# A two-layer decoder in one kernel: a shorter block table, ranks taken from logits, and the blocks' normalisation worked out in pairs

## The chip, the cores and the metric

One Trainium2 chip, one core. The metric is the device time of one execution in microseconds, the median of three executions: 1794.66 (1793.82 to 1794.86) for the kernel before. The profile that is quoted below comes from another execution of the same kernel, with a time of its own.

## The reference, cut to what matters

Thirty-two batches of 100 tokens with 256 features pass six stages. Every stage adds its input and ends in a layer norm without gain:

```python
x = _layernorm(x + _L0_attn_ref(x, ...), axis=-1)
x = _layernorm(x + _L0_xattn_ref(x, ctx_1024, ctx_1024, fside_BxSxS2_0, ...), axis=-1)
x = _layernorm(x + _L0_ffn_ref(x, ...), axis=-1)
x = _layernorm(x + _L1_attn_ref(x, ...), axis=-1)
x = _layernorm(x + _L1_xattn_ref(x, ctx_1024, ctx_1024, ...), axis=-1)
x = _layernorm(x + _L1_ffn_ref(x, ...), axis=-1)
```

The change is in the last stage, a mixture of eight experts of which each token takes one:

```python
logits = x_flat @ Wg + bg
probs = jax.nn.softmax(logits, axis=-1)
assignments = jnp.argmax(probs, axis=-1)
h = jnp.einsum('nd,edh->neh', x_flat, W1) + b1[None]
h = jax.nn.gelu(h, approximate=False)
eo = jnp.einsum('neh,ehd->ned', h, W2) + b2[None]
selected = jnp.take_along_axis(eo, assignments[:, None, None], axis=1)[:, 0, :]
w = jnp.take_along_axis(probs, assignments[:, None], axis=1)
out = (w * selected).reshape(N, T, d)
```

## The kernel before

**Two layers of attention, in slots.** Nearly all of the time goes into self-attention and cross-attention of 32 batches in two layers. Their work is written out by hand: `at(slot, place, do)` puts a step at one of four places of a slot, and `run_slots` (L677) issues slot after slot. The order of each engine's instructions is the order of these calls; no scheduler moves them.

**Routing, beside the last attention slots.** When a batch has left the second layer's cross-attention, `router` (L518) makes its logits. Batches are routed in groups of four; the last groups are 28 to 30, and 31 alone (`group_of`, L582). For each group `centred_logits` (L592) subtracts the largest logit, `exponentials` (L598) takes exp on ScalarE, and `one_hot` (L601) forms the shares and marks the expert with the largest one, by a product with `rank` so that one alone is marked. `ahead_of` (L615) adds the marks into `sofar`; `counted` (L622) counts on TensorE how many tokens of the same expert come before a token; `rows_of` (L627) makes a row number of that; `send` (L641) scatters the batch's rows with an indirect DMA from GpSimd into `regions` in DRAM, in which each expert has an area of its own. A row has 258 numbers: 256 features, the share, and the token's number.

**The block table.** `block_table` (L652) cuts the regions into 32 blocks of 128 rows. From the counts of the eight experts it works out, on all 128 partitions and for all 32 blocks along the free axis (128 x 256 elements), at which row each block begins and which expert it belongs to. The result is `table`, whose first partition is read into registers by SyncE, TensorE and VectorE.

**The blocks.** After the slots come the 32 blocks (L828). For block i, `load_block` (L778) reads two registers and loads the rows `xb` and the expert's first weights `wb`, ten blocks ahead; `turn_block` (L790) transposes on TensorE and copies on ScalarE (`bxT`), two ahead; `first_layer` (L798) makes four products and two Gelu activations (`bhT`), one ahead; `second_layer` (L809) makes the second product (`bo`) and then on VectorE adds the bias `b2` (L817), multiplies by the share and adds the residual (L818), and takes mean and variance (L77, L79); GpSimd works out the scale as (variance + margin) to the power -0.5 (L81, L82). `store_block` (L821) follows one block later: VectorE centres and scales (L86), and GpSimd scatters 128 rows into the output (L637). `b2`, 1 MB with its copies for all partitions, is loaded by SyncE ahead of the first block (L773). Each of the PSUM tiles of the blocks has two buffers; `xb` and `wb` have twelve.

The order on GpSimd is thus margin, power, scatter of the block before, margin, power, scatter, and so on. An engine runs its instructions in order: one that waits holds up all behind it.

Of the kernel before, what the change touches and what calls it, by code (L numbers as in the profile page):

```python
# [10 lines left out]
F32 = mybir.dt.float32  # L11
# [7 lines left out]
E = 8  # L19
# [5 lines left out]
GROUP = 4  # L25
ROW = D + 2
# [5 lines left out]
NO_TOKEN = 1.0e6  # L32
LAYER = (0, SLOTS * B + 23)
COLUMNS = ("parity", "l0s_bq", "l0s_bk", "l0s_bv", "l0x_bq", "l0x_bk", "l0x_bv", "l1x_bq", "l1x_bk", "l1x_bv")
ROWS = ((("l0s_bo", D), ("l0x_bo", D), ("dscale", 1), ("ffn_g", D), ("ffn_b", D)),
        (("l1s_bo", D), ("l1x_bo", D), ("bg", E), ("rank", E), ("base", E), ("order", BLOCKS)))
# [20 lines left out]
def decoder_kernel(ctx: ExitStack, tc: tile.TileContext, a: dict, out: bass.AP):  # L57
# [10 lines left out]
    table = state.tile([P, 2, BLOCKS], I32, name="table")  # L68
# [19 lines left out]
    with ExitStack() as att:  # L88
# [21 lines left out]
        nc.vector.tensor_copy(x_all[:, :, D + 1], ids)  # L110
        no_token = const.tile([P, ROW], F32, name="no_token")
        nc.gpsimd.memset(no_token, 0.0)
        nc.gpsimd.memset(no_token[:, D + 1:], NO_TOKEN)
# [341 lines left out]
        def plan_batch(l, b):  # L455
# [103 lines left out]
            if l == 0:  # L559
                at(start + 8, 2, keep("ln_n", lambda: layer_norm_scale(sm, xs[b], 0.001, "n", f"n_{b}")))  # L560
                at(start + 9, 3, feed_forward_input)
                at(start + 11, 3, lambda: transpose_rows(t["xn"], "n", tag, dst=xnT[:, :, b, :]))
            else:
                at(start + 9, 0, keep("x3T", lambda: transpose_rows(xs[b], "m", tag)))
                at(start + 11, 1, router)
                first, n = group_of(b)
                if b == first + n - 1:
                    for do, s, place in ((centred_logits, 11, 3), (exponentials, 12, 1), (one_hot, 12, 3),
                                         (ahead_of, 13, 3), (counted, 15, 0), (rows_of, 15, 3)):
                        at(start + s, place, lambda do=do: do(first, n))  # L570
                    for i in range(n):
                        at(start + 16 + i, 1, lambda i=i: send(first + i))
# [9 lines left out]
        def group_of(b):  # L582

            if b == B - 1:
                return b, 1
            first = b // GROUP * GROUP
            return first, min(GROUP, B - 1 - first)

# [3 lines left out]
        def centred_logits(first, n):  # L592
            routed["col"] = sm.tile([S, GROUP], F32, tag="col", name=f"col_{first}")[:, :n]
            lg = routed["lg"] = routed["logits"][:, :n, :]
            nc.vector.tensor_reduce(routed["col"], lg, AX.X, ALU.max)
            nc.vector.tensor_tensor(lg, lg, over_experts(routed["col"]), ALU.subtract)
# [4 lines left out]
        def one_hot(first, n):  # L601

            lg, col = routed["lg"], routed["col"]
            nc.vector.tensor_reduce(col, lg, AX.X, ALU.add)
            nc.vector.reciprocal(col, col)
            nc.vector.tensor_tensor(lg, lg, over_experts(col), ALU.mult)
            top = x_all[:, first:first + n, D]
            nc.vector.tensor_reduce(top, lg, AX.X, ALU.max)
            hot = routed["hot"] = w2.tile([S, GROUP, E], F32, tag="hot", name=f"hot_{first}")[:, :n, :]
            nc.vector.tensor_tensor(hot, lg, over_experts(top), ALU.is_equal)  # L610
            nc.vector.tensor_tensor(hot, hot, c["rank"][:S].unsqueeze(1).to_broadcast([S, n, E]), ALU.mult)
            nc.vector.tensor_reduce(col, hot, AX.X, ALU.max)
            nc.vector.tensor_tensor(hot, hot, over_experts(col), ALU.is_equal)
# [38 lines left out]
        def block_table():  # L652

            ps = bank("counts")[:, :E]
            nc.tensor.matmul(ps, lhsT=ones[:S, :], rhs=sofar, start=True, stop=True)
            full = w1.tile([P, E, B], F32, tag="full", name="full")
            nc.vector.tensor_tensor(full[:, :, :PER_EXPERT], ps.unsqueeze(2).to_broadcast([P, E, PER_EXPERT]),
                                    c["order"][:, :PER_EXPERT].unsqueeze(1).to_broadcast([P, E, PER_EXPERT]), ALU.is_gt)
            n = sm.tile([P, E], F32, tag="tb_n", name="tb_n")
            nc.vector.tensor_reduce(n, full[:, :, :PER_EXPERT], AX.X, ALU.add)  # L660
            upto = sm.tile([P, E], F32, tag="tb_upto", name="tb_upto")
            nc.vector.tensor_copy(upto[:, 0:1], n[:, 0:1])
            for e in range(1, E):
                nc.vector.tensor_tensor(upto[:, e:e + 1], upto[:, e - 1:e], n[:, e:e + 1], ALU.add)
            nc.vector.tensor_scalar(upto, upto, float(P), None, ALU.mult)
            nc.vector.tensor_scalar(n, n, -float(P), float(B * S), ALU.mult, ALU.add)
            past = w1.tile([P, BLOCKS, E], F32, tag="past", name="past")
            nc.vector.tensor_tensor(past, c["order"].unsqueeze(2).to_broadcast([P, BLOCKS, E]),
                                    upto.unsqueeze(1).to_broadcast([P, BLOCKS, E]), ALU.is_ge)
            col = sm.tile([P, BLOCKS], F32, tag="tb_col", name="tb_col")  # L670
            nc.vector.tensor_reduce(col, past, AX.X, ALU.add)
            nc.vector.tensor_scalar(table[:, 1, :], col, float(E - 1), None, ALU.min)
            nc.vector.tensor_tensor(past, past, n.unsqueeze(1).to_broadcast([P, BLOCKS, E]), ALU.mult)
            nc.vector.tensor_reduce(col, past, AX.X, ALU.add)
            nc.vector.tensor_tensor(table[:, 0, :], col, c["order"], ALU.add)
# [77 lines left out]
        at(LAYER[1] + 2, 3, load_second_weights)  # L753
        for i in range(FILLS):
# [6 lines left out]
        run_slots()  # L761
        block_table()

    with ExitStack() as moe:
        mw = moe.enter_context(tc.tile_pool(name="mw", bufs=1))
        m2 = moe.enter_context(tc.tile_pool(name="m2", bufs=2))
        m4 = moe.enter_context(tc.tile_pool(name="m4", bufs=4))
        m12 = moe.enter_context(tc.tile_pool(name="m12", bufs=12))
# [3 lines left out]
        b2 = mw.tile([P, E, D], F32, name="b2")  # L772
        nc.sync.dma_start(b2, a["b2"].to_broadcast([P, E * D]).rearrange("p (e d) -> p e d", e=E))  # L773
        y_all = mw.tile([P, BLOCKS, D], F32, name="y_all")
        to_all = mw.tile([P, BLOCKS], I32, name="to_all")
        blocks = [{} for _ in range(BLOCKS)]

        def load_block(i):  # L778
            t = blocks[i]
            why = "the table's rows and experts are within these bounds for any counts"  # L780
            first = nc.values_load(table[0:1, 0, i:i + 1], engines=(mybir.EngineType.SP,), min_val=0,
                                   max_val=(BLOCKS_AT_MOST - 1) * P, skip_runtime_bounds_check_because=why)
            t["e"] = nc.values_load(table[0:1, 1, i:i + 1], engines=(mybir.EngineType.SP, mybir.EngineType.PE, mybir.EngineType.DVE),
                                    min_val=0, max_val=E - 1, skip_runtime_bounds_check_because=why)
            t["x"] = m12.tile([P, ROW], F32, tag="xb", name=f"xb_{i}")
            nc.sync.dma_start(t["x"], regions[bass.ds(first, P), :])
# [22 lines left out]
        def second_layer(i):  # L809
# [5 lines left out]
            nc.vector.tensor_copy(to_all[:, i:i + 1], t["x"][:, D + 1:])  # L815
# [86 lines left out]
```

## Time and profile before

| what | us |
|---|---|
| median of three executions | 1794.66 |
| time of the profiled execution | 1794.34 |
| its span, first to last instruction | 1792.6 |
| last batch's logits on VectorE (L525) | 1688.11 |
| block table's first step on VectorE (L657) | 1691.93 |
| last output of `block_table` (L675) | 1696.58 to 1696.77 |
| first block's transposes on TensorE (L794) | 1702.02 |
| first block's bias on VectorE (L817) | 1708.51 |
| last scatter of rows into the output begins | 1785.46 |

Read it from the outside in. TensorE is busy for 96% of the span, with a granted clock of 0.98 on average, and 85% of the chain that ended last is TensorE's: that is the two layers of attention. The last hundred microseconds are another matter: there TensorE has idle stretches, and the order of GpSimd and VectorE sets the pace. A column "idle before" tells how long an engine had nothing to do before a group, and the arrow whom it waited for; a time on the GpSimd line is rougher than on the others.

### The profile page before, as it was taken

What the parts mean: (1) busy time and instruction counts of PE and PEld (TensorE: products, weight loads), DVE (VectorE), ACT (ScalarE), POOL (GpSimd) and SP (SyncE); (2) the same over time, 40 slices, a digit from 0 to 9 for tenths busy, and PEclk for the clock granted to TensorE, in tenths of its full rate; (3) what the DMA queues carried; (4) which work ended last, traced back from release to release, by engine and by line L of the source; (5) the groups of instructions that cost most, each with busy time, mean ns of one, the idle gap of its engine ahead of it and who ended that gap; (6) DMA issues with size and microseconds to landing.
All of it is one profiled execution on the core that took longest, in us unless ns stands there. A gap on an engine that the chain in (4) does not pass through costs nothing.

```text
span 1792.6 us, 52296 instructions
## 1 busy us (share of the span) xinstructions
PE 1712.5 (96%) x20797; PEld 1303.7 (73%) x20797; DVE 1294.8 (72%) x3846; ACT 914.7 (51%) x2285; POOL 1114.9 (62%) x1685
## 2 busy tenths in 40 slices
PE   8999999999999999998899999999999999999595
PEld 6777777777777777776667777777777777776384
DVE  5667776777777776786577777877777777866576
ACT  3555555555555555554345555555555555554242
POOL 1565666666666666664166666676766666665467
PEclk9999999999999999999899999999999999999898
DMA  4000232233313231210100000000000000000182
GB/s 156 13 30 21 79 83 69 57 82 79 81 49 83 79 82 54 68 33 10 64 2 18 19 15 23 18 28 18 20 18 28 18 15 23 19 28 12 54 253 92
DMA packets 60592, 89.38 MB, mean 50 GB/s; under 512 B 5723, under 2 KB 43101, under 8 KB 60222
## 3 DMA queue, kind: packets, MB, share of 16 engines
q1 hardware_dynamic: 56334, 78.91, 15.6%
q0 software_dynamic: 3584, 6.59, 1.2%
q8 instruction: 165, 2.70, 0.6%
q14 instruction: 77, 0.63, 0.1%
q10 hardware_dynamic: 432, 0.53, 0.1%
HBM read 52.09 MB, written 34.84 MB: 48 GB/s over the span
## 4 chain that ended last, share of the span: by engine, by line
PE 85%; POOL 5%; DVE 5%; issue 2%; ACT 1%; DMA 0%; SPq 0%; POOLq 0%; DVEq 0%; ACTq 0%
PE r_t_x L362 15%; PE sc_x L265 11%; PE r_v L507 9%; PE r_k L496 9%; PE r_a_x L372 9%; PE r_t_s L319 5%; PE r_o_x L291 3%; PE r_a_s L326 3%; PE sc_s L265 3%; POOL pr L352 3%; PE r_o_s L291 3%; PE r_qx L245 2%; DVE pr L348 2%; PE r_n_s L275 2%; POOL out_dram L637 2%
## 5 line engine op out<-in xcount | busy, mean ns | idle before, releaser
L352 POOL TENSOR_TENSOR pr<-pr,mx_x 100x361 f32<-100x361 f32 x992 | 761.6, 798 | 480.1 <-DVE mx_x L348 476.6
L363 ACT ACTIVATE pT_x<-r_t_x 120x400 f32<-120x400 f32 (+1 forms) x768 | 380.3, 504 | 300.0 <-PE r_t_x L362 295.5
L362 PEld LDWEIGHTS r_t_x<-ident,pr 100*120 100x120 f32 (+1 forms) x3072 | 323.4, 138 | 143.2 <-issue 47.3
L362 PE MATMUL r_t_x<-ident,pr 100*120 100x100 f32 (+1 forms) x3072 | 398.0, 253 | 10.4 <-POOL pr L352 8.9
L348 DVE CUSTOM_DVE_ANT_0 pr<-sc_x,dist 100x361 f32<-100x361 f32 x512 | 244.5, 530 | 131.0 <-PE sc_x L265 80.1
L348 DVE CUSTOM_DVE_ANT_0 pr<-sc_x,zero 100x361 f32<-100x361 f32 x512 | 244.7, 530 | 116.6 <-PE sc_x L265 91.4
L265 PE MATMUL sc_x<-kT_x,qz_x 32*100 32x361 f32 x2048 | 222.0, 503 | 4.8 <-DVE mx_x L348 4.1
L372 PE MATMUL r_a_x<-pT_x,v_cross 120*32 120x100 f32 (+1 forms) x6144 | 185.8, 254 | 1.8 <-ACT kT_x L498 1.8
L320 ACT ACTIVATE pT_s<-r_t_s 100x400 f32<-100x400 f32 x256 | 118.7, 502 | 71.8 <-PE r_t_s L319 69.7
L372 PEld LDWEIGHTS r_a_x<-pT_x,v_cross 120*32 120x32 f32 (+1 forms) x6144 | 129.2, 110 | 33.8 <-ACT kT_x L498 3.0
L306 DVE TENSOR_REDUCE mx_s<-sc_s 100x16 f32<-100x1600 f32 x64 | 116.4, 1819 | 32.2 <-PE sc_s L265 31.5
L498 ACT ACTIVATE kT_x<-r_k,c_columns 128x361 f32<-128x361 f32 x128 | 72.1, 563 | 108.4 <-PE r_k L496 108.4
L309 DVE TENSOR_TENSOR pr_s<-sc_s,mx_s 100x1600 f32<-100x1600 f32 x64 | 116.8, 1824 | 2.2
L319 PE MATMUL r_t_s<-ident,pr_s 100*100 100x100 f32 x1024 | 116.7, 251 | 1.4 <-DVE pr_s L309 1.4
L319 PEld LDWEIGHTS r_t_s<-ident,pr_s 100*100 100x100 f32 x1024 | 99.9, 130 | 15.9 <-issue 4.9
L509 ACT COPY v_cross<-r_v 120x256 f32<-120x256 f32 (+1 forms) x192 | 71.5, 373 | 75.0 <-PE r_v L507 75.0
L507 PE MATMUL r_v<-shared,ctx 128*120 128x256 f32 (+1 forms) x384 | 101.4, 386 | 0.0
L265 PEld LDWEIGHTS sc_x<-kT_x,qz_x 32*100 32x100 f32 x2048 | 68.3, 160 | 45.3 <-issue 29.7
L507 PE MATMUL r_v<-c_l1x_wv,ctx 128*120 128x256 f32 (+1 forms) x384 | 101.1, 386 | 0.0
L496 PE MATMUL r_k<-ctx,c_l1x_wk 128*128 128x361 f32 x256 | 90.7, 477 | 0.0
L496 PE MATMUL r_k<-ctx,shared 128*128 128x361 f32 x256 | 89.0, 470 | 0.0
L348 DVE DVE_READ_ACCUMULATOR2_ANT mx_x<- 100x1 f32 x1024 | 84.1, 82 | 0.0
(217 smaller groups left out, 2770.9 us busy)
## 6 DMA issues: line engine op xcount, KB each, us to landing
regions<-no_token SPq DMA_DIRECT2D x23, 1161.0 KB
ctx<-in_ctxT_dram SPq DMA_DIRECT2D x64, 361.0 KB
wb<-in_experts_dram SPq DMA_DIRECT2D x32, 257.0 KB
dist<-in_dist_dram SPq DMA_DIRECT2D x32, 141.0 KB
xb<-regions SPq DMA_DIRECT2D x32, 129.0 KB
x_all<-in_x_dram SPq DMA_DIRECT2D x32, 100.0 KB
shared<-in_experts_dram SPq DMA_DIRECT2D x8, 256.0 KB
b<-in_b_dram SPq DMA_DIRECT2D x1, 1024.0 KB
```

Source lines behind the costliest of these rows:

```text
L265: nc.tensor.matmul(dst, lhsT=qz[rows, p, k, :], rhs=kT[rows, k, :], start=True, stop=True)
L306: nc.vector.tensor_reduce(mx, sg, AX.X, ALU.max)
L309: nc.vector.tensor_tensor(pr, sg, mx.unsqueeze(3).to_broadcast([S, NG, NG, S]), ALU.subtract)
L319: nc.tensor.transpose(pt[:, j, :], t["pr_s"][:, j, g, :], ident[:S, :S])
L320: nc.scalar.activation(t["pT_s"][:, g], pt, AF.Exp)
L348: nc.vector.tensor_tensor_reduce(pr[:, j, :SK], sc[:, j, :], bias, 1.0, LOWEST, ALU.add, ALU.max, mx)
L352: nc.gpsimd.tensor_tensor(pr[:, j, :SK], pr[:, j, :SK], mx.to_broadcast([S, SK]), ALU.subtract)
L362: nc.tensor.transpose(pt[:n, j, :], t["pr_x", g][:, j, k0:k0 + n], ident[:S, :S])
L363: nc.scalar.activation(t["pT_x", g][:n, i], pt[:n], AF.Exp)
L372: nc.tensor.matmul(av[32 * j:32 * j + 32, :], lhsT=t["v_x"][:n, i, head(g, j), :], rhs=t["pT_x", g][:n, i, j, :], start=(i == 0), stop=(i ...
L496: nc.tensor.matmul(ps, lhsT=c[sx + "_wk"][:, k, m * P:(m + 1) * P], rhs=t["ctx"][:, k, :], start=(k == 0), stop=(k == NC2 - 1))
L507: nc.tensor.matmul(ps, lhsT=t["ctx"][:, k, k0:k0 + n], rhs=c[sx + "_wv"][:, k, :], start=(k == 0), stop=(k == NC2 - 1))
```

## The change

**Routing.** The mark of the expert is taken from the logits themselves (`ranked`), before exp; the share of the largest is one over the sum of the exponentials (`shares`), which comes later. Batches 30 and 31 are now routed alone, 28 and 29 as a pair, and the slots and places of these last steps are written in `ROUTING`. **Block table.** The number of blocks of an expert is rounded with a large constant instead of counted; a running sum is one scan; and each block has a partition of its own (32 x 7 elements), after which one 32 x 32 transpose turns the two columns into two rows. **Biases.** `b2` is loaded some 30 slots before the second layer's end into the memory of `xnT`, which is no longer read by then. **Tables.** The Gelu table is loaded ahead of `block_table`. **Registers.** Four blocks' numbers are read at once. `xb` has sixteen buffers. **Blocks.** Mean and variance of all blocks are kept; GpSimd works out the scale of two blocks at once, with the scatters of an earlier pair between its instructions; VectorE makes a shift (-mean times scale) for the pair, and ScalarE applies scale and shift to each block. The last three blocks are normalised on VectorE. The token's numbers are integers, so the scatter reads them from `xb` without a copy.

```diff
+ROUTING = (((11, 1), ((11, 3), (12, 3), (13, 3), (15, 0), (15, 2), (15, 3), (16, 1))),
+           ((10, 3), ((11, 1), (11, 2), (11, 3), (12, 2), (12, 2), (13, 0), (13, 3))),
+           ((9, 1), ((9, 1), (9, 1), (9, 1), (9, 2), (9, 2), (9, 2), (9, 3))))
...
-                for do, s, place in ((centred_logits, 11, 3), (exponentials, 12, 1), (one_hot, 12, 3),
-                                     (ahead_of, 13, 3), (counted, 15, 0), (rows_of, 15, 3)):
+                for do, (s, place) in zip((ranked, exponentials, ahead_of, counted, shares, rows_of), steps_of_group):
                     at(start + s, place, lambda do=do: do(first, n))
...
-            if b == B - 1:
+            if b >= B - 2:
                 return b, 1
...
+        def ranked(first, n):
+            col = sm.tile([S, GROUP], F32, tag="col", name=f"col_{first}")[:, :n]
             lg = routed["lg"] = routed["logits"][:, :n, :]
+            nc.vector.tensor_reduce(col, lg, AX.X, ALU.max)
             hot = routed["hot"] = w2.tile([S, GROUP, E], F32, tag="hot", name=f"hot_{first}")[:, :n, :]
+            nc.vector.tensor_tensor(hot, lg, over_experts(col), ALU.is_equal)
+            nc.vector.tensor_tensor(lg, lg, over_experts(col), ALU.subtract)
             nc.vector.tensor_tensor(hot, hot, c["rank"][:S].unsqueeze(1).to_broadcast([S, n, E]), ALU.mult)
             nc.vector.tensor_reduce(col, hot, AX.X, ALU.max)
             nc.vector.tensor_tensor(hot, hot, over_experts(col), ALU.is_equal)
...
+        def shares(first, n):
+            top = x_all[:, first:first + n, D]
+            nc.vector.tensor_reduce(top, routed["lg"], AX.X, ALU.add)
+            nc.vector.reciprocal(top, top)
...
             ps = bank("counts")[:, :E]
+            nc.tensor.matmul(ps, lhsT=share_of_block, rhs=sofar, start=True, stop=True)
             n = sm.tile([P, E], F32, tag="tb_n", name="tb_n")
+            nc.vector.tensor_scalar(n, ps, 0.5 - 0.5 / P, ROUND, ALU.add, ALU.add)
+            nc.vector.tensor_scalar(n, n, ROUND, float(P), ALU.subtract, ALU.mult)
             upto = sm.tile([P, E], F32, tag="tb_upto", name="tb_upto")
+            nc.vector.tensor_tensor_scan(upto, ones[:, :E], n, 0.0, ALU.mult, ALU.add)
+            past = sm.tile([32, E - 1], F32, tag="tb_past", name="tb_past")
+            col = sm.tile([32, 2], F32, tag="tb_col", name="tb_col")
+            nc.vector.tensor_scalar(past, upto[:32, :E - 1], c["steps"][:32, 0:1], None, ALU.is_le)
+            nc.vector.tensor_reduce(col[:, 1:2], past, AX.X, ALU.add)
+            nc.vector.tensor_scalar(n, n, -1.0, float(B * S), ALU.mult, ALU.add)
+            nc.vector.tensor_tensor_reduce(past, past, n[:32, :E - 1], 1.0, c["steps"][:32, 0:1], ALU.mult, ALU.add, col[:, 0:1])
+            nc.vector.tensor_copy(rows_by_block[:, 0:64:32], col)
+            nc.vector.transpose(table, rows_by_block)
...
+        b2 = xnT.rearrange("p k b s -> p (k b s)")[:, :E * D].rearrange("p (e d) -> p e d", e=E)
+        at(LAYER[1] + SLOTS * B - 30, 3, lambda: nc.sync.dma_start(b2, a["b2"].to_broadcast([P, E * D]).rearrange("p (e d) -> p e d", e=E)))
...
         run_slots()
+        nc.scalar.preload_act_table_set("gelu_and_others")
         block_table()
...
-            nc.vector.tensor_copy(to_all[:, i:i + 1], t["x"][:, D + 1:])
-            t["ln"] = layer_norm_scale(m4, y, 1e-05, "b", f"b_{i}")
+            st = m4.tile([P, 6], F32, tag="st", name=f"st_{i}")
+            nc.vector.bn_stats(st, y)
+            nc.vector.bn_aggr(mv_all[:, i, :], st)
...
+        def margin(i, n):
+            nc.gpsimd.tensor_scalar_add(rs_all[:, i:i + n], mv_all[:, i:i + n, 1], 1e-05)
+        def scale(i, n):
+            nc.gpsimd.tensor_tensor(rs_all[:, i:i + n], rs_all[:, i:i + n], mhalf.to_broadcast([P, n]), ALU.pow)
+        def shift_of(i, n):
+            nc.vector.scalar_tensor_tensor(shift[:, i:i + n], mv_all[:, i:i + n, 0], -1.0, rs_all[:, i:i + n], ALU.mult, ALU.mult)
+        def normalise_on_scalar(i):
+            nc.scalar.activation(y_all[:, i, :], y_all[:, i, :], AF.Identity, bias=shift[:, i:i + 1], scale=rs_all[:, i:i + 1])
...
+        def finish_pair(i):
+            margin(i - 1, 2)
+            if i > 2:
+                store(i - 3)
+            scale(i - 1, 2)
+            if i > 2:
+                store(i - 2)
+        for i in range(-10, BLOCKS):
+            for f, d in ((load_block, 10), (turn_block, 2), (first_layer, 1)):
                 if 0 <= i + d < BLOCKS:
                     f(i + d)
...
+            if i % 2 and 2 < i < BLOCKS - 1:
+                shift_of(i - 3, 2)
+                for k in (3, 2):
+                    normalise_on_scalar(i - k)
+            if i == BLOCKS - 1:
+                normalise(i - 1)
+            second_layer(i)
+            if i == BLOCKS - 2:
+                margin(i, 1)
+                normalise(i - 2)
+                store(i - 2)
+                scale(i, 1)
+                normalise(i - 1)
+                store(i - 1)
+            elif i == BLOCKS - 1:
+                store(i - 1)
+                margin(i, 1)
+                scale(i, 1)
+                normalise(i)
+                store(i)
+            elif i % 2:
+                finish_pair(i)
```

## The prediction

> **What bounds the kernel now.** I first read the busy time by stage: columns are the stretch, its length, busy microseconds (and instructions) of TensorE, its weight loads, VectorE, ScalarE and GpSimd, TensorE's granted clock, the DMA share and GB/s.
>
> ```profile
> 855.00:1560.00 705.00, 688.73 (x8699) 520.50 (x8698) 532.43 (x1572) 365.66 (x907) 456.92 (x695) 0.99 0.07 21
> ...
> 1680.00:1706.00 26.00, 8.59 (x43) 7.29 (x43) 12.34 (x61) 2.20 (x7) 5.73 (x10) 0.61 0.36 116
> 1706.00:1786.00 80.00, 66.47 (x434) 58.01 (x433) 63.56 (x191) 31.93 (x95) 63.56 (x96) 0.95 0.60 182
> ```
>
> In attention TensorE is busy 98% of the time; what the change takes from VectorE there is under cover. From 1680 to 1706 TensorE works a third of the time: routing and table are a chain. From 1706 to 1786 come the blocks. The chain of waits shows the first stretch (start, length, what):
>
> ```profile
> 1692.32 0.37 DVE tb_n L660
> ...
> 1696.12 0.43 DVE tb_col L674
> ...
> 1696.65 0.33 SPq L773
> ...
> 1697.03 0.49 SPq L781
> ...
> 1698.25 0.36 SPq L786
> ```
>
> The table takes VectorE from 1691.93 to 1696.77; the 1 MB bias load is issued next, then registers are read and the first rows requested, 1.48 us behind the table. The order of time shows the blocks:
>
> ```profile
> 1726.50 0.24 POOL L81 TENSOR_SCALAR rs_b<-mv_b 128x1 f32<-128x1 f32 x1
> ...
> 1726.82 0.57 POOL L82 TENSOR_TENSOR rs_b<-rs_b,mhalf 128x1 f32<-128x1 f32 x1
> 1727.06 0.18 DVE L79 BATCH_NORM_AGGREGATE mv_b<-st_b 128x2 f32<-128x6 f32 x1
> ...
> 1727.43 0.41 DVE L86 TENSOR_SCALAR y_all<-y_all,mv_b,rs_b 128x256 f32<-128x256 f32 x1 [0.18 <-POOL rs_b L82]
> ...
> 1727.61 1.19 POOL L637 DMA_INDIRECT out_dram<-y_all,to_all  x1 [0.22 <-issue]
> ...
> 1728.84 0.25 POOL L81 TENSOR_SCALAR rs_b<-mv_b 128x1 f32<-128x1 f32 x1
> ```
>
> GpSimd never waits for data: 0.24 margin, 0.08 gap, 0.57 power, 0.22 gap, 1.19 scatter, 0.04 gap make 2.34 us a block (1726.50 to 1728.84), and VectorE waits for the power. TensorE's own lap is shorter: `bo` begins at 1711.40, 1713.38, 1715.36, so 1.975 us.
>
> **The change, part by part.** The sum goes against the profiled execution: 1794.34, which is the span of 1792.6 and 1.74 outside it; the median is 0.32 above it.
>
> *Ahead of the last ranking: +0.85.* In the built kernel's order two sends (28, 29) now stand on GpSimd in front of the margin and power of batch 31, where GpSimd was idle for 6.07 us before (L81 at 1684.15). A send is 0.19 cast, 0.30 gap, 1.03 scatter, 0.04 gap = 1.56, two 3.1. Their rows should be ready near 1682.0 (behind `o` of 31, at 1680.40 before and some 0.9 later, as the counting products precede it on TensorE, plus three steps of 0.2). GpSimd is then free at 1685.4 and the power done at 1686.35; VectorE's normalisation, at 1685.54 before, starts at 1686.4, and the router and everything behind it are late by that. Bounds: 0, if the rows are earlier, to +1.6.
>
> *Ranking: -0.88.* From the logits (L525, 1688.11) to the end of `sofar` (L620, 1690.80) before: ten VectorE steps, exp, then the counting pair. After: six steps and the pair; 8 x 0.205 (their spacing) = 1.64 to the last start, against 1690.63 - 1688.11 = 2.52. Exp and the share now hide behind the counting products.
>
> *Table: -2.7.* 4.84 us become ten small instructions. Nine at 0.205 and an accumulator read of 0.08 are 1.93. The scan, the product with a sum and the 32 x 64 transpose are in no row: from 0.15 (the smallest copy, L815) to 0.42 (L674, 128 x 256) each. They are small, so I take 0.28: 2.15 in all; bounds 1.8 to 2.6.
>
> *First load: -0.8.* Without the bias load SyncE starts reading 0.2 sooner; two reads of four registers cost between one read's 0.27 and four times that, and I add 0.1. The first rows took 3.74 us (1698.25 to 1701.99) behind 1 MB, the second 3.05: -0.7, bounds 0 and -1.7. They must wait for the last send: its row is ready about 1692.0 as before, the scatter ends at 1693.6, the request leaves about 1695.5, 1.9 later; the last output scatter had landed 1.7 us after its end (1786.43 to 1788.1, where SyncE's wait for it ended). So it is just hidden, at most 1.7 if not. The Trainium skill (DMA: Bandwidth & Descriptors, Anatomy of one DMA) gives a DMA about 2.0 us of fixed cost, most of it the confirmation of the write; by it the send would end the wait, some 0.1 later, and the sum would be 8.3.
>
> *Gelu table: -0.42.* It stood from 1705.63 to 1706.92; the first `bo` at 1707.34 also needs `bh` of block 1, which ends at 1706.92. Bounds 0 and -1.28.
>
> The first bias (1708.51) thus comes 0.85 - 0.88 - 2.7 - 0.8 - 0.42 = -3.95 sooner.
>
> *The blocks: -4.45.* GpSimd's own work for a pair falls to 0.24 + 0.57 + 2 x 1.19 and gaps, 3.7. But a new ring closes in which a scatter lies between margin and power. VectorE: shift 0.2 (a small step), then block i: 0.46 + 0.52 + 0.46 + 0.18 = 1.62 (starts of L817, L818, L77, L79, end). GpSimd: 0.09 handover (L79 to L81 when idle, 1712.11 to 1712.20), margin 0.24, 0.25 gap, scatter 1.15, 0.04, power 0.6, 0.04, and the next shift: 4.25 us a pair. Power on two columns is in no row: 0.57 as for one, or 1.14; I take 0.6, since a subtraction over 361 columns takes 0.80 (L352) and columns cost little. TensorE needs 3.95 a pair. ScalarE waits for the shift with the next `bxT` and Gelu queued behind, and TensorE for these; two Identity of about 0.51 (L478: 0.60 for 361 columns) put `bxT` 1.65 behind the shift, `bo` of the next pair's second block 5.5 behind, and VectorE wants it 5.9 behind: slack 0.4. From the first bias: 5.7 to the first shift (three laps), 13 rings of 4.25, and a tail. Tail, from the last shift to the last scatter: 4.15 to block 28's power, 3.7 for the next two scatters, a margin and a power of block 30, 0.45 normalisation, 1.62 block 31, 1.65 its margin, power, normalisation and handover: 11.55. In all 72.5, before 1785.46 - 1708.51 = 76.95.
>
> *Hidden.* The bias load of 1 MB lies near slot 313, in a stretch with a DMA share of 0.06 to 0.07; on SyncE only `ctx` loads queue behind it, five slots ahead of use; without cover it is the 3.2 us that 1 MB takes at the 332 GB/s seen at 1698. Two more GpSimd fills at the start (0.1 to 0.2 each) end before 4.8, and GpSimd's next work is at 19.89. Loads now press harder on DMA (share 0.8 to 0.9 at 250 GB/s): 0.39 MB a block at 300 is 1.3 us, below the ring's 2.1.
>
> Sum: -3.95 - 4.45 = -8.4. The profiled time would be 1785.9, the median 1786.3.
>
> **Rivals.** *TensorE becomes the bound.* If the ring is below 3.95, TensorE's lap sets the pair: another 13 x 0.3 = 3.9 off, 1782.4. For it: the scatter lasts 0.97 where VectorE is idle (the last one) against 1.19; L86 leaves VectorE. Against: VectorE is still busy 3.4 of 4.25. The Trainium skill (GPSIMD Engine Reference, Specifications) says GpSimd shares its SBUF interface with VectorE and contends with instructions that have two SBUF inputs or a two-port mode; the trace's 1.19 against 0.97 agrees, but L818 with its two SBUF inputs stays.
>
> *The front gives its gain back*: sends later, a longer first load. Then only the blocks gain: 1794.66 - 4.45 = 1790.2. For it: the two sends in front of batch 31's scale.
>
> *The power costs by the column.* 0.57 more in 13 rings and the tail is +8.0: 1794.3, no change; the change would not do on GpSimd what it says.
>
> *Slower: ScalarE's wait starves TensorE.* If TensorE has nothing ready while ScalarE stands at the shift, a pair is 1.65 + 3.95 = 5.6: +17.6, so 1803.9. It loses from a ring of 4.9 (8.4 / 13 above 4.25). For it: two PSUM buffers, a slack of 0.4. Against: two blocks' products lie ready ahead of the shift.
>
> **How the numbers follow.** Forecast 0.42, TensorE bound 0.20, front given back 0.14, power 0.12, starvation 0.12. A measurement here tells 0.2%, 3.6 us, from no change. Faster: 0.42 + 0.20 + most of 0.14 = 0.74; same: 0.12 and the rest, 0.14; slower 0.12. The range goes from 1780 (TensorE bound, all of the bias load's 1.7 and the table's 1.28) to 1793.5 (nearly the doubled power), and leaves starvation out.
>
> **What would show it.** The table's last step some 2.7 earlier than 1696.77 and the first bias near 1704.6; power on two columns near 0.6; shifts 4.25 apart, each waiting for GpSimd; ScalarE's Identity waiting for the shift, TensorE hardly idle. Wrong: shifts 4.9 or more apart, or a power of 1.1; a first load that waits for a send's landing.

## The result, and the profile after

| | before | after |
|---|---|---|
| median, us | 1793.98 (22 runs) | 1790.78 (22 runs) |
| the profiled execution | 1794.34 | 1788.15 |
| its span | 1792.6 | 1785.9 |

The ratio is 0.9982, with a 95% interval of 0.9974 to 0.9990: 3.2 us less (1.8 to 4.7), where 8.4 were forecast. A second comparison of the same two kernels (`after_again`) gave 0.9980 (0.9969 to 0.9991). The two profiled executions differ by 6.2 us, nearly twice as much as the medians; why is told below, and it decides how a profile of this kernel may be used.

Between fixed points of the program the traces can be laid side by side (us, from the trace's instruction times):

| stretch | before | after |
|---|---|---|
| start to the first cross-attention output product (L291; L299 after) | 93.39 | 94.50 |
| to the 129th, at the start of the second layer | 847.38 | 842.73 |
| to the 241st | 692.24 | 692.27 |
| to the last batch's logits (L525; L533) | 55.09 | 57.55 |
| to the first block's bias (L817; L829) | 20.40 | 15.48 |
| to the start of the last scatter | 76.95 | 76.18 |
| to the end | 7.10 | 7.22 |

The first two lines and the third are code that the change hardly touches, and yet they hold 3.5 of the 6.7 us by which the spans differ.

**The front.** The chain of waits of the changed kernel, start, length, what (SPq is SyncE's queue):

```profile
1689.86 0.18 POOL place L649
1690.04 0.61 issue
1690.65 2.76 DMA regions<-x_all,place
...
1693.69 0.35 SPq L799
```

From the cast on, no step of the table stands in this chain. The table's last step starts at 1691.33 and is done by 1691.56. The first request for rows leaves at 1693.69, when the last send (issued at 1690.65) has landed. Here the new chain has become last send, landing, first rows.

**The blocks.** One ring of the changed kernel in order of time (start, length, engine, line, operation, tiles; in brackets the idle time before and who ended it):

```profile
1722.17 0.16 DVE L842 SCALAR_TENSOR_TENSOR shift<-mv_all,rs_all 128x2 f32<-128x2 f32 x1 [1.16 <-POOL rs_all L839]
1722.29 0.42 DVE L829 TENSOR_TENSOR y_all<-bo,xnT 128x256 f32<-128x256 f32 x1
...
1723.73 0.18 DVE L833 BATCH_NORM_AGGREGATE mv_all<-st 128x2 f32<-128x6 f32 x1
...
1724.01 0.22 POOL L836 TENSOR_SCALAR rs_all<-mv_all 128x2 f32<-128x2 f32 x1 [0.65 <-DVE mv_all L833]
...
1724.81 1.02 POOL L644 DMA_INDIRECT out_dram<-y_all,xb  x1 [0.58 <-ACT bxT L809]
...
1725.86 0.74 POOL L839 TENSOR_TENSOR rs_all<-rs_all,mhalf 128x2 f32<-128x2 f32 x1
...
1728.47 0.22 POOL L836 TENSOR_SCALAR rs_all<-mv_all 128x2 f32<-128x2 f32 x1 [0.65 <-DVE mv_all L833]
```

The ring is the predicted one: shift, a block on VectorE, margin, scatter, power, next shift; VectorE waits 1.16 for the power and GpSimd 0.65 for VectorE, so neither is full. But it takes 4.46 (margins at 1724.01 and 1728.47), against 4.25 forecast and the 2 x 2.34 of before.

**The end of attention.** Stretches of 5 us of the kernel before and of the changed one (columns as in the prediction's first fence; the last but two is TensorE's granted clock):

```profile
1670.00:1675.00 5.00, 4.12 (x55) 3.01 (x54) 4.28 (x18) 1.27 (x4) 3.65 (x5) 1.00 0.00 0
1675.00:1680.00 5.00, 3.85 (x68) 2.63 (x66) 2.10 (x7) 2.81 (x8) 2.54 (x5) 1.00 0.01 3
```

```profile
1670.00:1675.00 5.00, 3.86 (x46) 2.81 (x44) 3.84 (x15) 2.42 (x7) 3.81 (x6) 0.87 0.01 3
1675.00:1680.00 5.00, 4.58 (x44) 3.62 (x40) 2.07 (x12) 0.81 (x3) 0.18 (x1) 0.50 0.01 2
```

In the changed kernel TensorE works its last products of attention at half clock: from 1675 to 1680 it is busier and does 44 products instead of 68. In the kernel before, the clock falls when attention is over (at 1685.5). Changed kernels whose clock stays full here take 55.60 to 55.66 for this stretch, so the half clock is some 1.9 of the 2.46 us lost in the fourth line of the table; the rest lies in VectorE's order (below, `rank_later`).

### The profile page after: what moved, and what is told of

It reads as the page before. It is cut to its first block, busy times and chain, and to the rows that moved or that the text cites. A ratio compares the mean times of both kernels' runs of the same rounds, so it can differ in the third digit from the quotient of the medians.

```text
span 1785.9 us, 52179 instructions
## 1 busy us (share of the span) xinstructions
PE 1710.4 (96%) x20801; PEld 1301.2 (73%) x20801; DVE 1278.5 (72%) x3785; ACT 925.2 (52%) x2314; POOL 1100.3 (62%) x1657
## 4 chain that ended last, share of the span: by engine, by line
PE 85%; POOL 5%; DVE 4%; issue 2%; DMA 2%; ACT 1%; SPq 1%; POOLq 0%; DVEq 0%; ACTq 0%
PE r_t_x L370 15%; PE sc_x L273 11%; PE r_v L515 9%; PE r_k L504 9%; PE r_a_x L380 9%; PE r_t_s L327 5%; PE r_o_x L299 3%; PE r_a_s L334 3%; PE sc_s L273 3%; PE r_o_s L299 3%; PE r_qx L253 2%; POOL pr L360 2%; PE r_n_s L283 2%; DVE pr L356 2%; PE r_n_x L283 2%
## 5 line engine op out<-in xcount | busy, mean ns | idle before, releaser
L356 DVE CUSTOM_DVE_ANT_0 pr<-sc_x,dist 100x361 f32<-100x361 f32 x512 | 244.5, 530 | 131.1 <-PE sc_x L273 80.2
L356 DVE CUSTOM_DVE_ANT_0 pr<-sc_x,zero 100x361 f32<-100x361 f32 x512 | 244.6, 530 | 112.0 <-PE sc_x L273 86.4
L356 DVE DVE_READ_ACCUMULATOR2_ANT mx_x<- 100x1 f32 x1024 | 83.9, 82 | 0.0
```

The costliest lines, as they stand in the source:

```text
L356: nc.vector.tensor_tensor_reduce(pr[:, j, :SK], sc[:, j, :], bias, 1.0, LOWEST, ALU.add, ALU.max, mx)
```

## The experiments

Times are medians; the kernel before was run beside them on the same chip each time (1794.6, 1791.7, 1791.9 and 1795.2 on four chips), so the ratios count.

| run | what | median (runs) | ratio to the kernel before |
|---|---|---|---|
| front_only | new front, old blocks | 1789.92 (11) | 0.9980 (0.9969 to 0.9991) |
| blocks_only | old front, new blocks | 1796.31 (12) | 1.0005 (0.9994 to 1.0017) |
| scale_first | power behind margin | 1784.47 (5) | 0.9953 (0.9941 to 0.9966) |
| no_preload | no early Gelu table | 1791.55 (11) | 0.9989 (0.9979 to 0.9999) |
| rank_later | ranking steps two slots later | 1784.89 (5) | 0.9960 (0.9947 to 0.9974) |
| b2_late | biases meant to load late | 1787.61 (4) | 0.9978 (0.9963 to 0.9992) |
| bias_behind_table | the same, second attempt | 1787.48 (1) | one execution |
| bias_in_front | the same, behind the table's reads | 1791.56 (10) | 0.9983 (0.9969 to 0.9996) |
| no_last_send | batch 31 not sent | 1787.15 (1) | one execution |
| warm | idle products on TensorE | 1786.21 (7) | 0.9970 (0.9959 to 0.9981) |
| after_again | the changed kernel | 1788.83 (12) | 0.9980 (0.9969 to 0.9991) |
| best1 | three edits together | 1778.22 (5) | 0.9921 (0.9908 to 0.9935) |
| best3 | three edits, another choice | 1780.05 (6) | 0.9925 (0.9904 to 0.9946) |

### Which half of the change pays: front_only, blocks_only

The first has the changed kernel up to `first_layer` and the end of a block from the kernel before (a copy of the token's number kept); the second has the blocks' end of the changed kernel on the kernel before, with integer numbers and sixteen buffers for `xb`.

> The front of the changed kernel (ranking, table, early bias load, Gelu table, reads of four registers) with the blocks' end of the kernel before: margin, power and scatter a block, normalised on VectorE. Theory 1 (the front pays what its profile shows, the blocks' ring is the term that was mis-sized): from the last batch's logits to the first bias 15.5 us as in the changed kernel (20.4 before), then a block in 2.34 us and 76.9 from the first bias to the start of the last scatter; the time is 4.9 below the kernel before, less 0.4 outside the span: near 1789.5. Rival (the moved routing steps give the gain back at the end of attention): the same 15.5, but the last logits come 3 us or so later against the stretch before 1670, and the time is within 2 us of the kernel before.

> Ranking, routing slots, table, bias load and register reads of the kernel before; only the blocks are as in the changed kernel (margin and power for a pair, normalised on ScalarE, index read straight from the block's rows). Theory 1: from the last logits to the first bias 20.4 us as before; rings of 4.46 us a pair, 76.2 from the first bias to the start of the last scatter, so 0.8 us below the kernel before, near 1793.2. The prediction's own sizes: rings of 4.25, 72.5, so 4.4 below. Rival (the moved routing steps cost at the end of attention): this kernel, which has not moved them, is as fast as the changed kernel or faster.

The front alone makes all of the gain (0.9980 against 0.9982), the new blocks alone make none (1.0005, where 0.8 us less was expected). Their profiles say the same: 15.86 us from the last logits to the first bias in the one, 20.79 in the other; 76.62 and 77.44 from there to the last scatter, where the kernel before has 76.95 (blocks_only needs 1.3 more than the changed kernel: four of its scatters last 1.16 to 1.28, where the changed kernel's last at most 1.09, and some of its rings take 4.7 to 4.9; why they are longer is open). The rival holds in part: the end of attention took 57.48 in front_only, as in the changed kernel, and 55.10 in blocks_only.

### What holds the blocks' ring: scale_first

```diff
             margin(i - 1, 2)
-            if i > 2:
-                store(i - 3)
             scale(i - 1, 2)
             if i > 2:
+                store(i - 3)
                 store(i - 2)
```

> The changed kernel with the pair's power right behind its margin and both scatters behind it (margin, power, store, store instead of margin, store, power, store). Theory 1 (the scatter between margin and power is what holds the ring at 4.46): the ring falls to some 2.9 us, below TensorE's 3.95 a pair, which then sets the pace: pairs 3.95 to 4.0 apart, 7 us less than the changed kernel, near 1784. Rival (ScalarE's wait at the shift or GpSimd's own work sets the pair): pairs stay over 4.3 apart and the gain is under 2 us.

GpSimd in order of time:

```profile
1730.79 0.22 POOL L836 TENSOR_SCALAR rs_all<-mv_all 128x2 f32<-128x2 f32 x1 [0.39 <-issue]
1731.09 0.72 POOL L839 TENSOR_TENSOR rs_all<-rs_all,mhalf 128x2 f32<-128x2 f32 x1
1732.00 1.07 POOL L644 DMA_INDIRECT out_dram<-y_all,xb  x1 [0.19 <-ACT bxT L809]
1733.37 0.97 POOL L644 DMA_INDIRECT out_dram<-y_all,xb  x1 [0.30 <-ACT y_all L845]
1734.74 0.22 POOL L836 TENSOR_SCALAR rs_all<-mv_all 128x2 f32<-128x2 f32 x1 [0.40 <-issue]
```

The pair now takes 3.95, TensorE's lap of two blocks; the stretch from the first bias to the last scatter falls from 76.18 to 68.92. The next two lines are the stretch 1705 to 1765, of this kernel and of the changed one: TensorE busy for 58.29 instead of 57.10 of 60 us, with 410 instead of 385 products.

```profile
1705.00:1765.00 60.00, 58.29 (x410) 53.45 (x408) 46.93 (x136) 40.72 (x115) 41.97 (x57) 1.00 0.71 218
```

```profile
1705.00:1765.00 60.00, 57.10 (x385) 50.14 (x384) 42.49 (x123) 37.20 (x108) 37.47 (x52) 1.00 0.68 207
```

So the scatter between margin and power was the ring, and neither ScalarE's wait at the shift nor GpSimd's own work was. The ratio, 0.9953, is the forecast size of the whole change, reached only with two more lines exchanged.

### What is lost at the end of attention: rank_later

```diff
-ROUTING = (((11, 1), ((11, 3), (12, 3), (13, 3), (15, 0), (15, 2), (15, 3), (16, 1))),
+ROUTING = (((11, 1), ((13, 2), (13, 3), (14, 1), (15, 3), (15, 3), (16, 0), (16, 1))),
```

> The changed kernel with the six ranking steps of batches 28 and 29 (and the same steps of all other groups of four) moved two slots later, behind the last row maxima of attention, and the counting and row steps behind them likewise. Theory 2 (these six VectorE steps, 1.25 us in front of the last four row maxima, hold GpSimd's subtraction and the last transposes up by 0.57 and leave TensorE's clock window there at 0.67 busy, on the edge at which the clock falls to half): from the 241st first product of the cross-attention output to the last batch's logits 55.1 us as in the kernel before, where the changed kernel has 55.7 without the early half clock and 57.5 with it; the time is 0.6 to 2.4 below the changed kernel, near 1789. Rival (the two sends of batches 28 and 29 on GpSimd delay batch 31's scale, as the prediction had it): no change, or later still, since these sends move later too.

VectorE in the changed kernel, and in rank_later:

```profile
1668.35 0.15 DVE L533 TENSOR_TENSOR logits<-r_l,c_rows 100x8 f32<-100x8 f32 x1
1668.54 0.17 DVE L605 TENSOR_REDUCE col<-logits 100x2 f32<-100x16 f32 x1
...
1669.63 0.17 DVE L611 TENSOR_TENSOR hot<-hot,col 100x16 f32<-100x16 f32 x1
1669.75 0.54 DVE L356 CUSTOM_DVE_ANT_0 pr<-sc_x,zero 100x361 f32<-100x361 f32 x1
```

```profile
1665.92 0.15 DVE L533 TENSOR_TENSOR logits<-r_l,c_rows 100x8 f32<-100x8 f32 x1
1666.65 0.54 DVE L356 CUSTOM_DVE_ANT_0 pr<-sc_x,zero 100x361 f32<-100x361 f32 x1 [0.57 <-POOL pr L360]
```

In the changed kernel the last row maxima of attention (L356) start 1.40 behind these logits, since the ranking of batches 28 and 29 stands in between; here 0.73. The stretch from the 241st output product to the last logits is 54.62 (54.31 and 54.51 in the two kernels below that have the same edit), 55.09 and 55.10 with the old routing. The ten profiles with the new routing show 55.60 to 55.66 six times, 56.00 once and 57.48 to 57.55 three times. The steps where the change put them thus cost 0.55 against the kernel before, and the half clock, where it comes early, 0.4 to 1.9 more; two slots later the steps cost nothing, and the stretch is 0.5 to 0.8 shorter than before. The gain in time, 0.9960 against 0.9982, is 3.9 us (2.7 beside b2_late, on the same chip), more than the 0.6 to 2.4 expected, with intervals that touch. Part of it lies where the expectation did not look: the edit also moves the steps of all other groups of four, and the stretch from the 129th to the 241st product takes 688.4 to 688.5 in the three profiles with it, against 689.7 to 689.8 in the five without it on the same two chips. The rival, the sends on GpSimd, falls: they were moved later still.

Why does the clock fall early in some executions? The clock's records switch only at multiples of 3.413 us from one another: in the kernel before at 839.0, 859.5, 873.1, 910.7 and 1685.5, which are 6, 4, 11 and 227 steps apart, and where this grid lies against the program differs from one execution to the next. In a window of that length around the ranking steps TensorE is busy for 0.67 of the time in the changed kernel (0.80 before), and after that window the clock fell in the three executions in which it began 40.8 to 41.3 us behind the 241st product, not in those in which it began 39.7 to 40.6 behind it; in one at 41.6 it fell a window later. The grid agrees with the Trainium skill (TensorE: Matmul & The Clock Gate, Part 1, What's actually happening), which has a free-running window of 3413 ns. The Trainium skill, in the same section, has half the clock after an idle window; here none of these windows was idle, so there the measurement decides. The busy share of one window does not decide it either: the clock held after windows of the same 0.67 in no_preload, b2_late, no_last_send and warm, and in best3 it fell after one of 0.80. What makes it fall stays open. So does whether the change makes it fall more often: three of ten profiles with the new order have it there, neither of the two with the old order, and both rank_later and best3 show one half-clock window earlier in the stretch (at 1646.8 and 1652.4).

### What the first load waits for: no_last_send, b2_late, bias_behind_table, bias_in_front, no_preload

> The changed kernel without the last scatter into the regions: the rows of batch 31 are not sent, so their output rows are left out; the counts, the table and the number of blocks are the same. Theory (the first request waits for that scatter's landing, 6.35 behind the last logits): the request moves up to where the table and the register reads allow it, 5.9 to 6.1 instead of 6.57, and the first rows with it by 0.5 to 0.7. Rival (the reads of the table end the wait): the request stays at 6.5 or later.

```diff
-                    for i in range(n):
+                    for i in range(n if b < B - 1 else 0):
                         at(start + s + i, place, lambda i=i: send(first + i))
```

The chain of waits of no_last_send:

```profile
1689.75 0.24 DVE table L676
1690.01 0.51 SPq L787
...
1691.32 0.35 SPq L799
```

Now the table and SyncE's reads stand in front of the first request. It leaves 5.78 behind the last logits (1691.32 - 1685.54), against 6.64 in the changed kernel (1693.69 - 1687.05): the wait for the landing costs the request 0.86. (The expectations count from the first of its preparing steps, 0.07 sooner.) The scatter ends 4.61 behind the logits and its landing shows at 6.35, 1.74 later. Yet the first bias came at 15.77 behind the logits, within the 15.48 to 16.31 of kernels that send batch 31 (`warm`, below, shows what stood in the way).

b2_late and bias_behind_table were to load the biases behind the table. They missed: nothing in the load waits for the table, so SyncE issued it as soon as it came to it, in the second one at 8.9 us ahead of the last logits. Both are repeats of the changed front: first bias 15.88 and 15.75 behind the logits.

> The changed kernel with the 1 MB of second biases loaded where the kernel before loads them, right behind the table. Theory (the first load waits for the last send's landing until 1693.5, so that SyncE's time is free, but 1 MB is then in front of it on the DMA engines): from the last logits to the first bias 1.0 to 1.7 us more than the 15.5 of the changed kernel. The prediction's size: 0.2 on SyncE and 0.7 in flight, 0.9 more. If the load were hidden in both places: 15.5.

> The changed kernel with the second biases in a tile of the blocks' own stage, as in the kernel before, so that their 1 MB can only be requested when attention's memory comes free, behind the table. Theory (in the changed kernel the first rows wait for the last send's landing, 6.35 behind the last logits; the bias load is then in front of them on the DMA engines): first rows requested at 6.6 to 7.0 behind the last logits, in flight 3 to 3.7 instead of 2.1, and the first bias 1.0 to 1.7 later than the 15.5 to 15.9 of kernels that differ from it only elsewhere. The prediction's size: 0.9 later. If this load is hidden as well: 15.5 to 15.9.

> The changed kernel with the second biases requested on SyncE behind the reads of the table and right in front of the first rows, which is what two earlier kernels were meant to do and did not. Theory (the first rows wait for the last send's landing anyway, so SyncE's time is free; the 1 MB then stands in front of them on the DMA engines): rows requested at 6.6 to 7.0 behind the last logits, first transposes 3 to 3.8 later instead of 2.2, first bias at 16.5 to 17.5 behind the logits instead of 15.5 to 16.1. Prediction's size: 0.9 later. Rival (at half clock TensorE's own products set the first bias, as without the last send, so that the biases cost nothing): 15.5 to 16.3.

Here the load is placed in `load_block(0)` behind the register reads, in SyncE's own order. SyncE's queue:

```profile
1688.85 0.33 SPq L797 DMA_DIRECT2D xnT<-in_b_dram  x1
1689.81 0.35 SPq L800 DMA_DIRECT2D xb<-regions  x1
```

The request for rows leaves at 6.64 as before, but the first transposes come at 11.39 instead of 8.8, and the first bias at 17.64. The early load is worth 1.3 to 2.2 us of the front (15.48 to 16.31 in kernels with it), and nearer to 1.3 where the clock is alike (below, `warm`).

> The changed kernel without the early load of the Gelu table, which then stands before the first Gelu. Theory 1 (hidden there): ScalarE is free from the second bxT copy on, 1.5 us ahead of the end of the first bh, so the load costs the first bias 0.1 us or less, and no time that can be told. Rival (the prediction's term): the first bias comes 0.4 to 1.3 us later.

Without the early Gelu table ScalarE shows:

```profile
1702.41 1.28 ACT L819 ACT_TABLE_LOAD   x1 [1.44 <-DMA xb<-regions]
1703.70 0.63 ACT L819 ACTIVATE bhT<-bh,wb 128x128 f32<-128x128 f32 x2
```

Theory 1's reason was wrong: the load is not hidden ahead of the first Gelu. It waits for the same product as the Gelu (first `bh` ended 12.73 behind the logits, the load began at 12.88) and the first Gelu comes 1.1 later than in the changed kernel. The first bias lies at 16.29 behind the logits, but kernels with the early load show 15.48 to 16.31, so its price on the path is between 0 and 0.8; beside kernels with a like clock (below, `warm`) it is near 0.1, as TensorE is then still at the second block's `bh` (1702.64 to 1704.55).

### What sets the first bias then: warm

```diff
         block_table()
+        for k in range(7):
+            nc.tensor.matmul(bank("warm")[:, :256], lhsT=ident, rhs=c["l1s_wo"].rearrange("p k d -> p (k d)")[:, :256], start=True, stop=True)
```

> The changed kernel with seven products of 128x256 that nobody reads behind the table's count on TensorE, where it is idle from 1689.6 to 1695.8. They compute nothing of the output. Theory 3 (the half clock that the records grant until 1701 is there because TensorE was idle, and costs the first blocks their time): the clock is full by 1697, the first products of bh take 1.06 instead of 1.92 us and the first bias comes 1.5 to 2 us sooner, 13.5 to 14 behind the last logits. Rival (the granted clock follows something else than TensorE's own work): 15.5 as before, or more, if the idle products are still running when the first rows land.

First products of the changed kernel, and of warm:

```profile
1697.57 0.69 PE L807 MATMUL bt<-ident,xb 128*128 128x128 f32 x2 [1.08 <-DMA xb<-regions]
1698.05 1.92 PE L817 MATMUL bh<-bxT,wb 128*128 128x128 f32 x8
```

```profile
1687.67 6.17 PE L768 MATMUL r_warm<-c_l1s_wo,ident 128*128 128x256 f32 x14
...
1695.72 0.44 PE L809 MATMUL bt<-ident,xb 128*128 128x128 f32 x2 [1.20 <-DMA xb<-regions]
1695.99 1.06 PE L819 MATMUL bh<-bxT,wb 128*128 128x128 f32 x8
```

Products that nobody reads bring the clock up before the rows land (full from 8.29 behind the logits, first transposes at 8.83): 1.06 instead of 1.92 us for the same products (each product of f32 shows as two). The first bias comes 14.89 behind the logits: 0.6 to 1.4 sooner than in kernels without them, less than expected, as the rows of the third block are then late (TensorE waits 0.91 for them). In time, 0.9970 against 0.9980 to 0.9982, the intervals overlap.

At half clock it is TensorE that sets the first bias. It works without a pause from the first `bh` to the first `bo`, and the first bias follows the point at which the full clock returns: 13.9 behind the logits in the changed kernel (first bias 15.48), 15.0 in b2_late (15.88), 15.9 in rank_later (16.31). The second block's `bh` of the changed kernel, and of no_last_send:

```profile
1700.18 1.45 PE L817 MATMUL bh<-bxT,wb 128*128 128x128 f32 x8
```

```profile
1697.99 1.91 PE L817 MATMUL bh<-bxT,wb 128*128 128x128 f32 x8
```

In no_last_send the clock stayed half until 15.3, so the rows that came 0.86 sooner were worked on at half clock for longer. On a line through b2_late and rank_later its 15.77 is about 0.25 early, no_preload's 16.29 (full clock from 15.6) about 0.1 late; bias_in_front's 17.64 (16.3) is 1.3 behind rank_later. These are single executions, so the sizes are estimates.

### The edits together: best1, best3, and the changed kernel again

> Three edits on the changed kernel together: the pair's power right behind its margin, the ranking steps moved as in rank_later, and the weights of blocks 0 and 1 requested ahead of the first rows, in the time in which SyncE waits for the last send to land. If the last wait is where the theory has it, the second rows are requested 0.5 sooner and the first bias comes 0.5 sooner, 15.0 behind the last logits. With 7.0 from the pair and 0.6 to 2.4 from the ranking steps: 1780.5 to 1783. If the edits hide one another: near 1784.5.

> The changed kernel with the pair's power right behind its margin, the ranking steps two slots later, and the seven unread products behind the table's count; the weights stay behind the rows. If the three add up: 54.3 to 54.7 from the 241st output product to the last logits, 14.9 from there to the first bias, 68.9 to the last scatter: 1 below best1, near 1777 where the kernel before takes 1791.7 (ratio 0.9915).

> The changed kernel once more, unchanged, beside the kernel before on the same chip. If its structure is worth 3.5 (4.8 at the front, 0.8 in the blocks, less 0.6 and about 0.9 at the end of attention and 0.5 outside and behind the last scatter), the ratio is 0.9980; if the earlier comparison was luck of the half-clock spells, it lies nearer to 0.9955 or to 1.

Both combinations take 0.992 of the kernel before, about four times the gain of the change. best1's third edit did not do what it should: the two weight loads are issued while the send still lands, but the rows' request then leaves 0.47 later, the first transposes at 10.26, and the first bias is at 15.85, not 15.0. Nor did the idle products add up in best3 (15.43, not 14.9; the clock fell again at 1696.8 for one window of 3.41). best1's median came in below its 1780.5 to 1783, best3's above its 1777. What both share, the power behind the margin and the later ranking, carries the gain.

## The prediction, step by step

| step | predicted | measured |
|---|---|---|
| ahead of the last ranking | +0.85 | +0.55, and 0.4 to 1.9 more in four of ten profiles |
| last logits to first bias (ranking, table, first load, Gelu table) | -4.80 | -4.92 in the pair of profiles, -4.1 with the latest first bias of kernels with this front |
| first bias to last scatter | -4.45 | -0.77 |
| last scatter to the end; outside the span | 0 | +0.12; +0.5 (2.25 against 1.74) |

Over the kernels with this front the sum is about -4.5 to -3.7 where the clock falls late and up to 1.9 less where it falls early, and the median's -3.2 (-4.7 to -1.8) fits; the forecast of -8.4 does not.

**The blocks, wrong: "The blocks: -4.45", "4.25 us a pair".** The mechanism was right, its terms were too small. The gap between margin and scatter is 0.58, not 0.25; the power on two columns 0.74, not 0.6; the scatter 1.02, not 1.15, and the rest of the lap is a little shorter: 4.46. Thirteen rings take 58.7 instead of 55.25 (13 x 0.21 = 2.7, and the first one is 0.75 longer), the tail 11.95 instead of 11.55, the way to the first shift 5.5 instead of 5.7. The working took each gap from rows in which GpSimd had not waited ahead of the scatter. The rival "TensorE becomes the bound" needed a ring below 3.95; scale_first has it. What spoke for it did come: the scatter takes 1.02 to 1.04 in the ring, and 1.19 still in front_only, where VectorE normalises; but the index comes from another tile there too, so the cause is not isolated.

**"In attention ... what the change takes from VectorE there is under cover", wrong.** It looked at what was taken away and not at where the rest was put: six steps, 1.25 us together, stand in front of the last row maxima. **"Ahead of the last ranking: +0.85"** named another mechanism, and that one fell: the two sends ended at 1683.3, and batch 31's margin ran at 1683.71, 0.10 behind its variance.

**Ranking and table, right in size.** The ranking's last step now starts 1.35 behind the logits (1.64 forecast, -1.17 instead of -0.88), and the table ends at 1691.56, 2.99 behind `sofar`, where it took 5.97: -2.98 instead of -2.7. **"So it is just hidden, at most 1.7 if not", wrong:** the last send is not hidden; without it the request starts 0.86 sooner. The prediction had the landing right (1.74 behind the scatter's end, 1.7 forecast) but thought that the table would hold the request for 1.9; it holds it for 1.2 (5.78 against 4.61). The rule that it weighed against this, the Trainium skill's 2.0 us of fixed cost (DMA: Bandwidth & Descriptors, Anatomy of one DMA), named the outcome that came, a request that waits for the send; its size was 0.1 there and 0.86 here. **First load -0.8, too small:** the biases out of the way are worth 1.3 to 2.2, more than the 0.7 taken from the two flights seen before. **Gelu table -0.42:** 0 to 0.8, and near 0.1 beside executions with a like clock. That the four add up to -4.80 against -4.92 is luck: the parts miss on both sides, and the profile of the changed kernel has nearly the earliest first bias of all with this front.

**ScalarE starvation, power by the column:** neither. A power on two columns costs 0.74 against 0.57 for one. **The front gives its gain back:** its 1790.2 lies nearest to the median of 1790.78, but by the opposite mechanism: the front kept its gain and the blocks made next to none.

**The profiled time.** The prediction made its sum against one execution, 0.32 off the median. That was luck: the stretch from the 113th to the 129th output product, where all kernels run the same code, took 142.5 to 149.1 us in the fifteen profiles: up to 142.9 with two or three half-clock windows in it, 148.3 and more with seven or eight.

Left open: where the 0.5 outside the span come from (front_only has none of it, 1.72 to 1.82 as in the kernel before; blocks_only 1.91 to 2.00; both halves together 2.16 to 2.28), and what share of the executions has the early half clock (four of ten profiles).

## What to carry to other kernels

Follow every instruction that a change moves to its new neighbours, on each engine: six small steps moved ahead of the last row maxima cost time that the same steps behind them do not. In a ring over two engines, put the instruction that the other engine waits for first, and whatever only has to be done in front of nobody: the pair's power ahead of both scatters took 7 us off the blocks. Compare stretches between fixed points of two traces, not two spans: here 3.5 of 6.7 us came from code that was the same in both.

## What the runs showed that was not expected

- The clock of TensorE falls to half for whole windows of 3.41 us, on a grid that lies differently in each execution. In the turn from the first layer to the second the same code differs by 6.6 us between executions, and goes with the number of these windows; that is twice the effect that was measured here.
- The stretch from the 129th to the 241st output product shows no half-clock window in any profile, and yet it takes 689.7 to 689.8 us with the changed kernel's order on two chips, 691.5 on a third and 691.9 to 692.3 on a fourth. Why is open; it is one more reason to compare on one chip.
- Seven products that nobody reads halve the time of the products behind them (1.92 to 1.06 us).
- In the blocks' ring and at the last send, a scatter on GpSimd starts 0.80 behind the start of a short instruction that had waited (margin at 1724.01, scatter at 1724.81; cast at 1689.86, scatter at 1690.65), whatever that instruction's own 0.2; behind the power, which is longer, the gap is 0.18.
